# Four graph layers on one core: permuted graph in place, running sums on VectorE for slots and counts, un-permuting in three bfloat16 parts

## The chip, the core and the metric

The kernel runs on one core of one Trainium2 chip. The metric is the device time of one execution in microseconds (us), lower is better. The core has five engines that run side by side, each working through its own queue in order: TensorE (PE, matmuls into PSUM; its weight loads are listed as PEld), VectorE (DVE), ScalarE (ACT), GpSimd (POOL) and SyncE (SP, which here only starts DMAs). Before the change the median of three runs is 2626.49 us (2620.58 to 2630.43).

## What is computed

32 graphs of 512 nodes with 64 features (`x`, 32x512x64) and weighted, sparse adjacency matrices (`adj`, 32x512x512) go through four layers. Each adds its result to its input and normalizes over the 64 features:

```python
x = _layernorm(x + _L0_gnn_ref(x, adj))                    # mean over neighbours
x = _layernorm(x + _L1_gnn_ref(x, adj, weight, bias))      # Chebyshev terms of the Laplacian
x = _layernorm(x + _L2_gnn_ref(x, adj, att_W, att_b))      # hyperbolic attention of all pairs
x = _layernorm(x + _L3_gnn_ref(x, adj, nodemask, W1, b1, W2, b2))
```

The change touches layer 3. It first thins out the neighbour lists (`_dilate_adj`), then takes for every node and feature a weighted sum of three quantiles (0.25, 0.5, 0.75) over the values of the node's remaining neighbours, and last a small dense network:

```python
agg = _weighted_nanquantile_agg(x, adj_d > 0)
h = relu((x + agg) @ W1 + b1);  y = h @ W2 + b2
```

## The kernel before

The work of a graph is cut into lanes, and the lanes of many graphs are under way at a time. P is 128, N is 512 nodes, T = N/P = 4 blocks of rows, D is 64.

*front* (line 882) loads the adjacency, transposes it, and does layers 0 and 1. *pairs* and *tail* (lines 969 to 1145) do layer 2 on all pairs of nodes; the result is `x3`, split into three bfloat16 parts `x3h` (line 757). *graph* (lines 786 to 876) makes the thinned adjacency as a 0/1 matrix `V` in fp16 (lines 809 to 828), and then `order` ranks the nodes by their number of neighbours and permutes the columns of V into that ranking: `perm` is a one-hot matrix, and four groups of four matmuls (line 857) give VP, one block of 128 rows at a time, which ACT copies out of PSUM (line 858). Then come the *slots*: for each node its running number within each column, that is a sum over all rows above it. Block j takes j matmuls with a constant matrix (all 2) over the blocks above and one with a triangular matrix (lines 860 to 864), so 1 + 2 + 3 + 4 matmuls of 128x512. The *counts* (lines 865 to 867) are four more with a matrix of ones.

*gather* (line 1147) turns slots into one-hot matrices `oh` on DVE and multiplies them with `x3h` on PE, so that slot s of every node holds the features of its s-th neighbour; the values go to two long tiles, `SB` (BODY, the nodes with few neighbours) and `SH` (HEAD, 32 columns with many neighbours for a pair of graphs). *sort* and *head* (lines 1239 and 1270) run sorting networks over the slots, which are tensor_tensor instructions of min and max on DVE (line 448), multiply the sorted values with weights of the three quantiles and sum. The result, still in the ranking's order, is `ap` (fp32, two graphs in one tile, line 1267). *finish* (line 1315) undoes the ranking: one-hot matrices `PT` in fp32, made by two ACT instructions each (line 485), and four fp32 matmuls for a graph (line 1340), each of which appears as two instructions in the trace; `dense` (line 1346) does the small network. For the last two graphs `spots` (line 1296) makes the one-hots early, in tiles of the lane *pairs*.

What sets the order: no engine order is written by hand. A planner, the class `Order` (line 181), records every operation with an engine, a modelled duration and its dependences, and then simulates the five engines (`issue`, line 295). Whenever an engine is free it takes, of the operations whose inputs are there, the one with the earliest due time. Due times come from `STAGES` (line 1415): for each lane the first and last due time of its operations, in periods of 80 us after the graph's number times 80 us (line 1478). On PE an operation that needs another shape of the array than the one before (64 or 128 rows, 64 or 128 columns) is put back by `STAY` (line 188), 51.0 us of due time. Buffers are part of the plan: an operation that needs a tile waits until a buffer of its tag is free. The order found is then fixed for each engine. Where the plan has PE idle, padding matmuls of zeros (`stay_active`, line 1451) are put in.

The tiles concerned: in *graph* the tags `nbT` (then `perm`), `v` (then `VP`), `V` and `junk` have one buffer of 128x2048 or 128x512 fp16 each; `col` (line 707) gives small 128x4 columns with two buffers. `tt`, `ts` and `stt` (lines 447 to 455) are DVE instructions, `act` (line 477) ACT, `mm` (line 491) PE.

Of the kernel before, what the change touches and what calls it, by code (L numbers as in the profile page):

```python
# [20 lines left out]
P = 128  # L21
# [10 lines left out]
K = 24  # L32
# [148 lines left out]
class Order:  # L181
# [3 lines left out]

    ENGINES = ("PE", "DVE", "ACT", "POOL", "SP")
    HOP = 0.1
    STAY = 51.0

    def __init__(self, nc, tc):  # L190
        self.nc, self.tc = nc, tc
# [212 lines left out]
def tile_adj_resnorm(ctx: ExitStack, tc: tile.TileContext, x, adj, nodemask, w1k, b1k, att_w, att_b,  # L404
# [206 lines left out]
    onesb = const.tile([P, P], BF16, name="onesb")  # L611
    nc.vector.memset(onesb, 1.0)
    zero = const.tile([P, 2 * P], BF16, name="zero")
    nc.vector.memset(zero, 0.0)

    wk = const.tile([P, KO * D // P, D + 2], F32, name="wk")
# [88 lines left out]
        return a.unsqueeze(2).to_broadcast([P, T, n])  # L705

    def col(name):
        return seq.tile(pools["small"], [P, T], F32, name, 2)

    def wide(name, tag=None):  # L710
        return seq.tile(pools["small"], [P, T, D], F32, name, 1, tag)
# [118 lines left out]
    def order(b, res):  # L830

        gm = pools["gm"]
        V = res["V"]
        key = col("key")
        stt(key, M3[:, b, :], float(N), iotr, op0=OP.mult, op1=OP.add)
        pt = bank()
        for t in range(T):
            tr(pt[:, t * P:(t + 1) * P], key[:, t:t + 1].to_broadcast([P, P]), identf)
        keyh = col("keyh")
        ts(keyh, key, -0.5, None, op0=OP.add)  # L840
        sg = col("sg")
        for t in range(T):
            junk = seq.tile(gm, [P, N], F16, "junk", 1)
            act(junk, pt, AF.Sign, bias=keyh[:, t:t + 1], scale=-1.0, accum_out=sg[:, t:t + 1])
        rk = col("rk")
        ts(rk, sg, -0.5, 0.5 * N - 1.0, op0=OP.mult, op1=OP.add)

        rkh = seq.tile(pools["keep"], [P, T], F16, "rkh", 8)
        cp(rkh, rk)
        perm = seq.tile(gm, [P, T, N], F16, "perm", 1, "nbT")  # L850
        for t in range(T):
            ts(perm[:, t, :], iotap, rk[:, t:t + 1], None, op0=OP.is_equal)
        VP = seq.tile(gm, [P, T, N], F16, "VP", 1, "v")
        for j in range(T):
            pt = bank()
            for t in range(T):
                mm(pt, V[:, t, j * P:(j + 1) * P], perm[:, t, :], start=(t == 0), stop=(t == T - 1))
            act(VP[:, j, :], pt, AF.Copy)
        slot = seq.tile(pools["keep"], [P, T, N], F16, "slot", 2)
        for j in range(T):  # L860
            pt = bank()
            for k in range(j + 1):
                mm(pt, UC[:, :P] if k == j else UC[:, P:2 * P], VP[:, k, :], start=(k == 0), stop=(k == j))
            act(slot[:, j, :], pt, AF.Copy)
        pt = bank()
# [16 lines left out]
    def front(b, res):  # L882
# [69 lines left out]
        pt = bank()[:, :T * (D + 2)].rearrange("p (t n) -> p t n", n=D + 2)  # L952
        nu = KO * D // P
        for t in range(T):
            mm(pt[:, t, :], onesb, bias1, start=True, stop=False)
# [314 lines left out]
    def head(b, res):  # L1270
# [19 lines left out]
        for g in range(2):  # L1290
            mm(pt[P - CUT:, g * P:(g + 1) * P], PRS[:, g:g + n - 1:2], identf, start=True, stop=True)
        act(ap[P - CUT:, :, 1, :], pt[P - CUT:, :2 * P].rearrange("p (g c) -> p g c", g=2), AF.Copy)
        for g in range(2):
            finish(b - 1 + g, res["ends"][g], ap[:, g], res["spots"][g] if b == B - 1 else None)

    def spots(ends):

        mid = pools["mid"]
        seq.lane = "pairs"
        home = seq.tile(mid, [P, 4, N], F32, "ends", 1, "Q")  # L1300
        ones = [seq.tile(mid, [P, 4, N], F32, f"ones{g}", 1, tag) for g, tag in enumerate(("EX", "RW"))]
# [12 lines left out]

    def finish(b, end, ap, spot):
        rk, x3 = end
        if spot:
            ones, home = spot
            po = bank(home=home and "pairs")
            for u in range(2):  # L1320
                for h in range(2):
                    mm(po[h * D:(h + 1) * D, :], ap[:, u, h * D:(h + 1) * D], ones[:, 2 * h + u], start=(u == 0),
                       stop=(u == 1 and h == 1), pair=True)
# [9 lines left out]

        po = bank()
        for u in range(2):
            PT = seq.tile(pools["fin"], [P, 2, N], F32, "PT", 1)
            for h in range(2):
                onehot(PT[:, h, :], rr, nposc[:, 2 * h + u:2 * h + u + 1], pools["fin"])
            for h in range(2):
                mm(po[h * D:(h + 1) * D, :], ap[:, u, h * D:(h + 1) * D], PT[:, h, :], start=(u == 0),  # L1340
                   stop=(u == 1 and h == 1), pair=True)
# [4 lines left out]
    def dense(po, x3T, x3, dst, nm, home=None):  # L1346
# [12 lines left out]
        act(hT, ph[:HID, :], AF.Relu, bias=b1s)  # L1359
        py = bank(home=lane)[:, :T * D].rearrange("p (t n) -> p t n", n=D)  # L1360
        for t in range(T):
            mm(py[:, t, :], onesb, bias2, start=True, stop=False)
# [8 lines left out]
    limits = const.tile([B, 2, K + 1], F32, name="limits")  # L1371
# [12 lines left out]
    def within_bounds():  # L1384
# [17 lines left out]
        for i, op in enumerate((OP.is_gt, OP.is_lt)):  # L1402
# [300 lines left out]
```

## Time and profile before

| | |
|---|---|
| median of three runs (lowest, highest) | 2626.49 us (2620.58, 2630.43) |
| profiled execution: time, span | 2622.02 us, 2620.2 us |
| busy: PE, PEld | 2458.2 us (94%), 1635.4 us (62%) |
| busy: DVE, ACT, POOL | 2402.7 us (92%), 1879.2 us (72%), 815.8 us (31%) |
| granted PE clock, mean | 0.982 |
| padding matmuls of line 1453 | 973, 132.9 us |
| sorting network, SB and SH (line 448, DVE) | 565.8 us and 347.4 us |
| gather matmuls (PE) | 5376, 516.5 us |
| permuting, perm by V (PE) | 512, 141.0 us |
| slots, VP by UC, and counts, VP by onesP (PE) | 320, 91.2 us, and 128, 33.1 us |
| un-permuting, PT by ap (PE, fp32) | 240, 111.2 us |

How to read it: a group's line gives the source line (often that of a helper), the engine, the operation, the tiles written and read, their shapes, the count, the busy time in us and the mean length of one in ns, and then the idle time of the engine just before and what ended it. Busy times of groups that overlap can't be added. Tiles carry their lane's name in front: `graph_VP`, `head_PT`, `sort_ap`. The span is the time from the first to the last instruction of the profiled execution; 1.8 us lie around it.

### The profile page before, as it was taken

The page shows a single profiled execution, that of the slowest core. Times are in us where ns is not written, and L with a number is a line of the kernel's source. Part 1 is how long each engine was busy: PE and PEld are TensorE (multiplying, and loading weights), DVE is VectorE, ACT ScalarE, POOL GpSimd, SP SyncE. Part 2 cuts the span into 40 slices and gives each one's busy share as a digit, 9 for nine tenths or more (in the row PEclk, how much of TensorE's full clock was granted, in tenths as well). Part 3 has the DMA queues.
Part 4 walks back from the last instruction along what each step waited for, and adds up shares of the span by engine and source line. Part 5 has one row for each costly group of instructions (what it writes and reads, how often), then busy time and mean ns, then how long its engine had stood idle before and what let it go on. Part 6 is the DMA issues. An engine that isn't in the chain of part 4 may idle for free.

```text
span 2620.2 us, 55667 instructions
## 1 busy us (share of the span) xinstructions
PE 2458.2 (94%) x19641; PEld 1635.4 (62%) x19667; DVE 2402.7 (92%) x9002; ACT 1879.2 (72%) x4406; POOL 815.8 (31%) x1783
## 2 busy tenths in 40 slices
PE   7999999999999999999999999999999999999997
PEld 6666566666666666666656666566666666666655
DVE  3668998999999999999999999999999999998996
ACT  5666677767777777767777677777777778776761
POOL 1233332332343333322333233333323333332210
PEclk9999999999999999999999899999999999998999
DMA  1100000000000000000000000000000000000000
GB/s 38 33 23 21 17 14 15 25 22 23 18 11 22 20 25 21 24 17 13 20 21 25 19 19 13 20 23 22 26 19 13 18 19 26 19 11 3 5 7 8
DMA packets 119723, 49.96 MB, mean 19 GB/s; under 512 B 53740, under 2 KB 119436, under 8 KB 119436
## 3 DMA queue, kind: packets, MB, share of 16 engines
q1 hardware_dynamic: 118272, 46.15, 6.4%
q8 instruction: 156, 2.56, 0.4%
q14 instruction: 131, 1.07, 0.1%
q10 hardware_dynamic: 1164, 0.18, 0.0%
HBM read 37.93 MB, written 8.39 MB: 18 GB/s over the span
## 4 chain that ended last, share of the span: by engine, by line
DVE 72%; PE 18%; ACT 6%; issue 2%; POOL 2%; DMA 0%; ACTq 0%; DVEq 0%
DVE SB L448 17%; DVE SH L448 8%; DVE gather_oh L452 6%; PE front_bank L502 5%; DVE pairs_Q L448 4%; PE gather_bank L502 3%; PE graph_bank L502 3%; DVE pairs_RW L448 3%; PE pairs_bank L502 3%; DVE sort_prod L448 3%; DVE pairs_Wt L455 3%; DVE pairs_L L455 2%; DVE tail_v L448 2%; DVE pairs_EX L448 2%; DVE pairs_RW L455 2%
## 5 line engine op out<-in xcount | busy, mean ns | idle before, releaser
L448 DVE TENSOR_TENSOR SB<-SB 128x448 f32<-128x448 f32 (+11 forms) x1424 | 565.8, 424 | 12.2 <-ACT SB L483 0.7
L502 PE MATMUL gather_bank<-gather_oh,tail_x3h 128*64 128x448 f16 (+5 forms) x5376 | 516.5, 321 | 4.8 <-ACT SB L483 3.4
L502 PEld LDWEIGHTS <-tail_x3h 128*64 128x64 bf16 x5376 | 296.0, 111 | 214.3 <-issue 112.8
L448 DVE TENSOR_TENSOR SH<-SH 128x32 f32<-128x32 f32 (+11 forms) x1744 | 347.4, 246 | 8.1
L502 PE MATMUL pairs_bank<-pairs_FT 67*128 67x512 f32 (+7 forms) x768 | 316.9, 516 | 18.7 <-ACT pairs_EX L483 7.1
L452 DVE TENSOR_SCALAR gather_oh<-graph_slot 128x256 f16<-128x256 f16 (+9 forms) x864 | 252.3, 337 | 25.3 <-PE gather_bank L502 23.5
L502 PE MATMUL front_bank<-front_AT,front_y 128*64 128x512 f32 x768 | 189.5, 607 | 18.5 <-DVE front_y L448 17.0
L502 PEld LDWEIGHTS pairs_bank<-pairs_FT 67*128 67x128 f32 (+1 forms) x768 | 130.2, 194 | 83.2 <-issue 19.7
L502 PE MATMUL graph_bank<-graph_perm,graph_V 128*128 128x512 f16 x512 | 141.0, 382 | 16.1 <-DVE graph_perm L452 13.8
L502 PEld LDWEIGHTS <-graph_nbT 128*128 128x128 f16 x1536 | 113.1, 99 | 57.6 <-issue 17.3
L722 POOL TENSOR_TENSOR front_rs<-front_var,mhalf 128x4 f32<-128x4 f32 x64 | 83.4, 1303 | 201.8 <-DVE front_var L452 152.9
L502 PEld LDWEIGHTS front_bank<-XA,front_AT 128*128 128x128 f32 x1024 | 126.0, 194 | 13.6 <-issue 6.3
L1453 PE MATMUL PA<-zero 128*128 128x256 bf16 x973 | 132.9, 278 | 0.1
L502 PE MATMUL pairs_bank<-FLS,pairs_Wt 128*128 128x66 f32 x1024 | 124.7, 274 | 3.9 <-DVE pairs_Wt L455 3.8
L502 PEld LDWEIGHTS pairs_bank<-FLS,pairs_Wt 128*128 128x128 f32 x1024 | 120.6, 192 | 10.9 <-DVE pairs_Wt L455 7.8
L502 PE MATMUL front_bank<-XA,front_AT 128*128 128x65 f32 x1024 | 124.5, 274 | 0.0
L448 DVE TENSOR_TENSOR pairs_RW<-pairs_RW,pairs_EX 128x640 f32<-128x640 f32 x128 | 104.1, 815 | 18.7 <-ACT pairs_RW L483 18.4
L502 PEld LDWEIGHTS <-tabs 128*128 128x128 f16 x1296 | 78.3, 100 | 64.2 <-issue 54.9
L502 PEld LDWEIGHTS front_bank<-front_AT,front_y 128*64 128x64 f32 x768 | 54.5, 137 | 95.6 <-issue 63.0
L483 ACT ACTIVATE graph_VP<-graph_bank 128x512 f16<-128x512 f32 x128 | 75.5, 590 | 53.7 <-PE graph_bank L502 49.4
L483 ACT ACTIVATE SB<-gather_bank 128x448 f32<-128x448 f32 (+2 forms) x192 | 81.3, 438 | 43.4 <-PE gather_bank L502 43.0
L502 PE MATMUL head_bank<-head_PT,sort_ap 128*64 128x512 f32 x240 | 111.2, 608 | 0.1
(354 smaller groups left out, 6569.8 us busy)
## 6 DMA issues: line engine op xcount, KB each, us to landing
front_A<-in_adj_dram SPq DMA_DIRECT2D x128, 256.0 KB, 2.7
XA<-in_x_dram SPq DMA_DIRECT2D x32, 128.0 KB, 2.2
xs<-tail_x SPq DMA_DIRECT2D x32, 128.0 KB, 1.9
out_dram<-head_zo SPq DMA_DIRECT2D x31, 128.0 KB, 2.0
out_dram<-tail_ends SPq DMA_DIRECT2D x1, 128.0 KB, 2.1
wk<-in_L_gnn_weight_dram ACTq DMA_DIRECT2D x1, 64.0 KB, 3.0
w1s<-in_L_gnn_W_dram ACTq DMA_DIRECT2D x2, 32.0 KB, 2.0
attw<-in_L_gnn_att_W_dram ACTq DMA_DIRECT2D x2, 0.2 KB, 3.2
```

Source lines behind the costliest of these rows:

```text
L448: vec(lambda: nc.vector.tensor_tensor(out, a, b, op=op), out, [a, b])
L452: vec(lambda: nc.vector.tensor_scalar(out, a, s1, s2, op0=op0, **kw), out, [a], True, (s1, s2))
L455: vec(lambda: nc.vector.scalar_tensor_tensor(out, a, s, b, op0=op0, op1=op1), out, [a, b], False, (s,))
L483: 0.3, lambda: nc.scalar.activation(out, a, f, scale=scale, **kw), [out, accum_out], [a, after] + sc, table)
L502: return nc.tensor.matmul(out, w, a, start=start, stop=stop)
L722: seq.op("POOL", 0.8, 0.6, lambda: nc.gpsimd.tensor_tensor(y, v, mhalf, op=OP.pow), [y], [v])
L1453: return nc.tensor.matmul(PA[:, 2 * P:], zero[:, :P], zero, start=False, stop=False)
```

## The change

- **Permuted graph in place.** VP no longer has a tile: block j is written into the columns of V that the four matmuls of block j have just read. `perm` moves from nbT's buffer to v's.
- **Running sums.** The blocks above are summed on DVE in fp16 (into `junk`'s buffer, then into VP[0] and VP[1], which are no longer needed by then), so each slot block takes one matmul with the triangular matrix and at most one with the matrix of twos on the sum; the counts take one.
- **Un-permuting in three bfloat16 parts.** `ap` is split into three parts `aph` by three ACT copies and two DVE subtractions for a pair of graphs; PT and the early one-hots become fp16, and each fp32 matmul becomes three 16-bit ones. The operations no longer carry `pair=True`, which halved their modelled duration.
- **Room and small constants.** Twelve columns get one buffer in place of two; `onesb` gives way to `onesP`, `zero` is half as long and broadcast for padding; `limits` becomes fp16.
- **Planner.** `STAY` goes from 51.0 to 35.7, and all lanes get other due times.

```diff
-    STAY = 51.0
+    STAY = 35.7
...
-    zero = const.tile([P, 2 * P], BF16, name="zero")
+    zero = const.tile([P, P], BF16, name="zero")
...
     def col(name):
-        return seq.tile(pools["small"], [P, T], F32, name, 2)
+
+        once = name in ("two", "sq2", "al", "dn", "hx", "hx2", "rsn", "gam", "sn", "lp", "run", "uc")
+        return seq.tile(pools["small"], [P, T], F32, name, 1 if once else 2)
...
-        perm = seq.tile(gm, [P, T, N], F16, "perm", 1, "nbT")
+        perm = seq.tile(gm, [P, T, N], F16, "perm", 1, "v")
...
-        VP = seq.tile(gm, [P, T, N], F16, "VP", 1, "v")
+        def four(a):
+            return a.rearrange("p (t n) -> p t n", n=P)
+
+
+        VP = [V[:, :, j * P:(j + 1) * P] for j in range(T)]
...
-            act(VP[:, j, :], pt, AF.Copy)
+            act(VP[j], four(pt), AF.Copy)
...
+        sums = [None, VP[0], four(seq.tile(gm, [P, N], F16, "sums", 1, "junk")), VP[0], VP[1]]
         for j in range(T):
             pt = bank()
-            for k in range(j + 1):
-                mm(pt, UC[:, :P] if k == j else UC[:, P:2 * P], VP[:, k, :], start=(k == 0), stop=(k == j))
+            mm(four(pt), UC[:, :P], VP[j], start=True, stop=(j == 0))
+            if j:
+                mm(four(pt), UC[:, P:2 * P], sums[j], start=False, stop=True)
+                tt(sums[j + 1], sums[j], VP[j], op=OP.add)
             act(slot[:, j, :], pt, AF.Copy)
         pt = bank()
-        for k in range(T):
-            mm(pt, onesP, VP[:, k, :], start=(k == 0), stop=(k == T - 1))
+        mm(four(pt), onesP, sums[T], start=True, stop=True)
...
+        aph = seq.tile(pools["fin"], [P, 3, 2, 2, P], BF16, "aph", 1)
+        for q in range(3):
+            act(aph[:, q], ap, AF.Copy)
+            if q < 2:
+                tt(ap, ap, aph[:, q], op=OP.subtract)
         for g in range(2):
-            finish(b - 1 + g, res["ends"][g], ap[:, g], res["spots"][g] if b == B - 1 else None)
+            finish(b - 1 + g, res["ends"][g], aph[:, :, g], res["spots"][g] if b == B - 1 else None)
...
-            PT = seq.tile(pools["fin"], [P, 2, N], F32, "PT", 1)
+            PT = seq.tile(pools["fin"], [P, 2, N], F16, "PT", 1)
...
-            for h in range(2):
-                mm(po[h * D:(h + 1) * D, :], ap[:, u, h * D:(h + 1) * D], PT[:, h, :], start=(u == 0),
-                   stop=(u == 1 and h == 1), pair=True)
+            for q in range(3):
+                for h in range(2):
+                    mm(po[h * D:(h + 1) * D, :], ap[:, q, u, h * D:(h + 1) * D], PT[:, h, :], start=(u == 0 and q == 0),
+                       stop=(u == 1 and q == 2 and h == 1))
...
-    STAGES = {"front": (-0.6, -0.5), "pairs": (1.2, 1.3), "tail": (0.2, 1.5), "graph": (0.9, 1.0), "gather": (2.7, 2.9),
-              "sort": (4.5, 4.6), "head": (4.7, 5.6), "ends": (4.0, 4.5), "check": (3.4, 4.8)}
+    STAGES = {"front": (-0.7, -0.2), "pairs": (1.2, 1.4), "tail": (0.7, 1.2), "graph": (1.2, 1.5), "gather": (2.8, 3.3),
+              "sort": (4.8, 5.4), "head": (5.0, 6.0), "ends": (4.6, 4.8), "check": (2.6, 6.0)}
...
-                return nc.tensor.matmul(PA[:, 2 * P:], zero[:, :P], zero, start=False, stop=False)
+                return nc.tensor.matmul(PA[:, 2 * P:], zero, zero[:, 0:1].to_broadcast([P, 2 * P]), start=False, stop=False)
```

More of the change, by code (lines that the diff above doesn't have):

```diff
@@ L610, in tile_adj_resnorm @@
     nc.vector.memset(tiny, 1e-36)
-    onesb = const.tile([P, P], BF16, name="onesb")
-    nc.vector.memset(onesb, 1.0)
-    zero = const.tile([P, 2 * P], BF16, name="zero")
+    zero = const.tile([P, P], BF16, name="zero")
     nc.vector.memset(zero, 0.0)
@@ L954, in front @@
         for t in range(T):
-            mm(pt[:, t, :], onesb, bias1, start=True, stop=False)
+            mm(pt[:, t, :], onesP, bias1, start=True, stop=False)
             for u in range(nu):
@@ L1300, in spots @@
         home = seq.tile(mid, [P, 4, N], F32, "ends", 1, "Q")
-        ones = [seq.tile(mid, [P, 4, N], F32, f"ones{g}", 1, tag) for g, tag in enumerate(("EX", "RW"))]
+        ones = [seq.tile(mid, [P, 4, N], F16, f"ones{g}", 1, tag) for g, tag in enumerate(("EX", "RW"))]
         seq.lane = "tail"
@@ L1320, in finish @@
             for u in range(2):
-                for h in range(2):
-                    mm(po[h * D:(h + 1) * D, :], ap[:, u, h * D:(h + 1) * D], ones[:, 2 * h + u], start=(u == 0),
-                       stop=(u == 1 and h == 1), pair=True)
+                for q in range(3):
+                    for h in range(2):
+                        mm(po[h * D:(h + 1) * D, :], ap[:, q, u, h * D:(h + 1) * D], ones[:, 2 * h + u],
+                           start=(u == 0 and q == 0), stop=(u == 1 and q == 2 and h == 1))
             for t in range(T):
@@ L1335, in finish @@
         for u in range(2):
-            PT = seq.tile(pools["fin"], [P, 2, N], F32, "PT", 1)
+            PT = seq.tile(pools["fin"], [P, 2, N], F16, "PT", 1)
             for h in range(2):
                 onehot(PT[:, h, :], rr, nposc[:, 2 * h + u:2 * h + u + 1], pools["fin"])
-            for h in range(2):
-                mm(po[h * D:(h + 1) * D, :], ap[:, u, h * D:(h + 1) * D], PT[:, h, :], start=(u == 0),
-                   stop=(u == 1 and h == 1), pair=True)
+            for q in range(3):
+                for h in range(2):
+                    mm(po[h * D:(h + 1) * D, :], ap[:, q, u, h * D:(h + 1) * D], PT[:, h, :], start=(u == 0 and q == 0),
+                       stop=(u == 1 and q == 2 and h == 1))
         for t in range(T):
@@ L1361, in dense @@
         for t in range(T):
-            mm(py[:, t, :], onesb, bias2, start=True, stop=False)
+            mm(py[:, t, :], onesP, bias2, start=True, stop=False)
             mm(py[:, t, :], hT[:, t * P:(t + 1) * P], w2s, start=False, stop=True)
@@ L1370, in tile_adj_resnorm @@
     flag = const.tile([1, 1], I32, name="flag")
-    limits = const.tile([B, 2, K + 1], F32, name="limits")
+    limits = const.tile([B, 2, K + 1], F16, name="limits")
     for s in range(K + 1):
```

## The prediction

> **What bounds the kernel now.** I read the page's busy shares first, then the busy row of each engine, then the busy times in three stretches (filling of the pipeline, middle, end), then the waits inside the middle.
>
> ```profile
> PE 2458.2 (94%) x19641; PEld 1635.4 (62%) x19667; DVE 2402.7 (92%) x9002; ACT 1879.2 (72%) x4406; POOL 815.8 (31%) x1783
> ...
> PE   7999999999999999999999999999999999999997
> ...
> DVE  3668998999999999999999999999999999998996
> ```
>
> Two engines look full. PE's 94% holds something that isn't work: the matmuls of line 1453 are padding between the real ones. The answer by stretches, columns PE, PEld, DVE, ACT, POOL:
>
> ```profile
> 0.00:196.50 196.50, 177.22 (x1348) 130.00 (x1349) 106.43 (x394) 124.67 (x266) 46.47 (x182) 0.98 0.11 32
> 196.50:2489.00 2292.50, 2170.34 (x17328) 1431.76 (x17351) 2188.14 (x8130) 1700.69 (x4012) 754.03 (x1575) 0.98 0.07 19
> 2489.00:2620.20 131.20, 110.66 (x970) 73.66 (x970) 108.17 (x479) 53.85 (x128) 15.25 (x26) 0.95 0.03 8
> ```
>
> DVE idles 90.1 us while the pipeline fills, 104.4 in the middle (4.5%) and 23.0 at the end, 217.5 in all. In the middle PE idles 122.2 us, and the same stretches for line 1453 alone give 52.0 us of padding there (132.9 in the run): 174 us free (7.6%). So DVE is the tighter engine and PE a close second. Who waits for whom in the middle (us in total, times, longest):
>
> ```profile
> DVE gather_oh L452 <- PE gather_bank L502: 21.4, 16, 3.0
> DVE pairs_RW L448 <- ACT pairs_RW L483: 14.3, 13, 3.7
> DVE front_st L714 <- PE front_bank L502: 10.0, 24, 2.3
> DVE pairs_EX L455 <- PE pairs_bank L502: 6.7, 6, 3.2
> DVE pairs_L L455 <- PE pairs_bank L502: 6.3, 6, 1.8
> ```
>
> ```profile
> PE front_bank L502 <- DVE front_st L714: 20.7, 33, 1.9
> PE front_bank L502 <- DVE front_y L448: 15.2, 25, 1.9
> PE graph_bank L502 <- DVE graph_perm L452: 13.4, 20, 1.3
> ```
>
> Each waits for the other, in many short waits. All lines of the first list that name PE add up to 51 us, those that name ACT or POOL to 30; the rest of the 104 is gaps too small to be listed. The chain that ended last says the same:
>
> ```profile
> DVE 72%; PE 18%; ACT 6%; issue 2%; POOL 2%; DMA 0%; ACTq 0%; DVEq 0%
> ```
>
> [...] 24 gather matmuls of 448 columns at 64 output rows take 2.46 us near the end, 0.10 each[...]
>
> **The change, part by part.** Prices, by shape (busy, mean ns):
>
> ```profile
> L502 PE MATMUL graph_bank<-graph_VP,UC 128*128 128x512 f16 x320 | 91.2, 383 | 2.6 <-ACT graph_VP L483 1.9 <-ACT graph_slot L483 0.5
> L502 PE MATMUL head_bank<-head_PT,sort_ap 128*64 128x512 f32 x240 | 111.2, 608 | 0.1
> L448 DVE TENSOR_TENSOR pairs_Q<-pairs_RW 128x512 f32<-128x512 f32 x32 | 21.8, 680 | 0.1
> L448 DVE TENSOR_TENSOR gather_oh<-graph_slot,last 128x512 f16<-128x512 f16 x32 | 13.3, 414 | 0.0
> ```
>
> Instructions overlap, so a duration isn't what one takes from its engine. The timeline of DVE shows by how much (start, length):
>
> ```profile
> 1277.32 0.41 DVE L448 TENSOR_TENSOR graph_nbT<-graph_nbT,identb 128x512 f16<-128x512 f16 x1
> 1277.66 0.64 DVE L448 TENSOR_TENSOR SH<-SH 128x14 f32<-128x14 f32 x4
> ```
>
> The next starts 0.34 us after an fp16 sum of 0.41 us; after the fp32 one of the pairs stage at 1304.82 it starts 0.58 us later. On PE four 128x512 fp16 matmuls in a row (the counts, at 331.66) take 1.03 us where one takes 0.38, so 0.22 us each.
>
> *Running sums on DVE (added).* Three fp16 sums of 512 elements for each of 32 graphs, 96 x 0.34 = 32.6 us. *Splitting ap into three parts (added).* Two fp32 subtractions of 512 elements for each of 16 pairs of graphs, 32 x 0.60 = 19.2 us (0.60: between 0.58 and the 0.68 of the row). DVE gets 51.8 us more, to 2454. Nothing is taken off DVE. Bounds: 45 if subtractions hide better, 62 with whole durations.
>
> *Slots and counts (removed from PE).* Matmuls per graph go from 1+2+3+4 plus 4 to 1+2+2+2 plus 1, 14 to 8: 6 x 0.22 x 32 = 42 us. *Un-permuting (changed on PE).* The fp32 row is 240 instructions in 111 us for 30 graphs, 3.7 us of busy time each, some of it overlap of ends. Twelve 16-bit matmuls of 512 columns take its place: 1.4 us if the halves run side by side (12 x 0.10 x 512/448), 2.6 if not (12 x 0.22). Saved: 1.1 to 2.3 us a graph; I take 1.1, since the two halves become ready apart, so 33 us. PE loses 75 us together (60 to 110).
>
> *ACT (added).* Three copies of 512 elements for each pair; the nearest row, head_PT's write from SBUF, is 628 ns: 48 x 0.63 = 30 us, on an engine that is busy 72%. Covered: free time of 592 us in the middle; without that cover 30 us. The one-hots in fp16 keep their 512 elements, so nothing there.
>
> *New waits.* The matmuls of slots 1 to 3 and of the counts now wait for ACT's copy and a DVE sum; behind them on PE lies whatever the planner put there. Each sum waits for ACT's copy of a block with the rest of DVE's queue behind it; so does each subtraction. That is 5 places a graph where DVE can stall; the listed waits of the middle are now 91, with 81 us. Bounds: 0 (planned where inputs are long there) to 13 us (96 sums and 32 subtractions x 0.1); I take 5.
>
> *End.* For the last two graphs nothing hides the splitting: three copies and two subtractions in a chain, 3 x 0.63 + 2 x 0.68 + about 0.8 for four hand-overs = 4 us, less 0.5 us of cheaper matmuls: +3.5 us, inside the stretch that now idles 23.
>
> *Buffers, STAY and STAGES.* perm moves into v's buffer and VP into V's, so nbT is free a step earlier and V later; the graph stage is rarely waited for by DVE (graph_v 1.4, graph_key 0.8, graph_mi 0.8, graph_nbT 0.4 us in the middle), so at most 3 us gained; I take none. Twelve small columns lose their second buffer: 0 to 10 us, I take none. The planner's numbers change the whole order: a lower STAY means more changes of tile shape on PE, other due times move waits about. No row shows it; bounds are minus 30 us (a third of the middle's idle time) and plus 30; I take 0. The filling of the pipeline hangs on the first graph's latency (gather starts at 183 us on PE), which no part shortens: 90 us of idle time stay. The smaller constants (onesP, zero, limits) cost nothing: the same instruction counts.
>
> *What comes back.* A lighter PE answers earlier. PE loses 75 of some 2325 us of real work, and DVE waits for PE 51 us in the middle; as DVE always has more queued work than before, I take back half of these waits and a little: 30 us.
>
> Sum: 2622.0 (the profiled execution: span 2620.2 and 1.8 around it) + 51.8 + 5 + 3.5 - 30 = 2652; the chain of waits gives a second reading: 51.8 x 72/92 = 40 added along DVE's part, 75 x 18/94 = 14 taken from PE's, 30 x 6/72 = 2 for ACT, so +28 and 2650 with 2622. The profiled execution lies inside the runs (2620.6 to 2630.4), 4.5 us below the median of 2626.5. I forecast **2650 us**, 0.9% slower than the median.
>
> **Rivals.** *PE paces, and DVE's idle time collapses (faster).* DVE would have 2454 us of work plus 90 + 23 + 4 at the ends. With 30 us of idle time in the middle the time is 2454 + 117 + 30 + 2 = 2603. It decides from 40 us down (2613): more than six tenths of the middle's idle time must go. For it: 51 us of it are waits for PE, and stretches with little idle time exist. Against it: PE waits for DVE longer than DVE for PE, and the 30 us for ACT and POOL and the small gaps stay. *Exactly as much comes back as is added (no change):* idle time of 40 to 65 us in the middle, about 2625. *The new order scatters the waits:* the middle's idle time grows to 130 us: 2454 + 117 + 130 + 2 = 2703; for it speak the single buffers, the new waits, and that a plan made on modelled durations is fragile when one engine is nearly full. *The sums don't do what they should:* if the block views keep fp16 at single rate, each costs 0.60 like fp32, 96 x 0.26 = 25 us more: 2675.
>
> **How the numbers follow.** Forecast (2640 to 2665) 0.36; PE paces 0.28; no change 0.22; scattered 0.09; single rate 0.05. This measurement can tell about 0.5% from no change, that is 2613 to 2640. Faster 0.28, same 0.22, slower 0.36 + 0.09 + 0.05 = 0.50. The range of 2592 to 2690 leaves out a tenth below (an order that is also better) and a tenth above. The slower cases alone span 2640 to 2703.
>
> **What would show it.** In the profile after: DVE busy near 2454 and x9130; three fp16 sums a graph at about 414 ns and subtractions near 680; 96 matmuls less in the slots (x224) and 96 less in the counts (x32); no fp32 rows with ap; DVE's share in the middle at 96% or more. If the waits on gather_bank, front_bank and pairs_bank nearly vanish and DVE reaches 98%, the first rival holds. If DVE's busy time is right but its share falls, the order did it. A DVE busy time that does not grow by 45 to 62 us would break the first step.

## The result, and the profile after

The median after the change is 2600.78 us over four runs (2598.72 to 2604.69), against 2626.39 us over four runs of the kernel before (2620.58 to 2630.43). The ratio is 0.9906, 95% interval 0.9884 to 0.9928: faster by about 0.9%. The forecast was 2650 us, slower by 0.9%; the time lies inside the range of 2592 to 2690 and close to the first rival's 2603.

The profiled execution took 2600.4 us, its span is 2598.0 us, 22.2 less than before. The busy shares of the page after, and DVE's busy row:

```profile
PE 2431.4 (94%) x19596; PEld 1606.4 (62%) x19626; DVE 2438.0 (94%) x9129; ACT 1915.9 (74%) x4464; POOL 825.5 (32%) x1783
...
DVE  3669999999999999999999999999999999999996
```

DVE has 127 instructions and 35.3 us more, and its row has lost the 8s in the middle. The stretches (columns: length, then PE, PEld, DVE, ACT, POOL with their counts, then the granted PE clock, DMA share, GB/s):

```profile
0.00:196.50 196.50, 179.32 (x1371) 131.21 (x1373) 108.04 (x411) 124.64 (x268) 49.29 (x185) 1.00 0.12 32
196.50:2469.00 2272.50, 2147.90 (x17287) 1400.24 (x17310) 2224.42 (x8261) 1741.39 (x4087) 759.92 (x1576) 0.99 0.07 19
2469.00:2598.00 129.00, 104.16 (x942) 74.93 (x943) 105.50 (x459) 49.84 (x113) 16.25 (x24) 0.93 0.03 8
```

Length minus busy time gives DVE's idle time: 88.5, 48.1 and 23.5 us, where it was 90.1, 104.4 and 23.0. So the span's 22.2 us are 35.3 more of work and 57.4 less of idle time, and 56.3 of those are in the middle, where DVE is now busy 97.9%. Who DVE waits for in the middle, the three longest:

```profile
DVE front_st L714 <- PE front_bank L502: 8.1, 20, 0.6
DVE gather_oh L452 <- PE gather_bank L502: 6.1, 5, 2.2
DVE pairs_L L455 <- PE pairs_bank L502: 5.3, 4, 2.3
```

These three were 10.0, 21.4 and 6.3 us, and the waits for ACT in `pairs_RW` (14.3) and for `pairs_EX` (6.7) have gone from the head of the list. Of PE's waits for DVE these two have become longer (they were 15.2 and 13.4):

```profile
PE front_bank L502 <- DVE front_y L448: 22.8, 42, 1.5
PE graph_bank L502 <- DVE graph_perm L452: 20.5, 27, 1.5
```

The chain of work that ended last has moved to DVE as well (it was 72% DVE, 18% PE):

```profile
DVE 83%; PE 10%; ACT 2%; issue 2%; POOL 2%; DMA 0%; ACTq 0%; DVEq 0%
```

The groups of the new work, by shape:

```profile
L502 PE MATMUL head_bank<-head_PT,head_aph 128*64 128x512 f16 x360 | 87.0, 393 | 1.9 <-ACT head_PT L483 1.6
...
L502 PE MATMUL graph_bank<-graph_V,UC 128*128 128x512 f16 x192 | 63.3, 383 | 0.5 <-ACT graph_V L483 0.4
...
L502 PE MATMUL graph_bank<-graph_V,onesP 128*128 128x512 f16 x32 | 12.3, 384 | 0.0
...
L502 PE MATMUL graph_bank<-graph_sums,UC 128*128 128x512 f16 x32 | 12.1, 379 | 0.0
```

```profile
L483 ACT ACTIVATE head_aph<-sort_ap 128x512 bf16<-128x512 f32 x48 | 30.1, 627 | 7.9 <-DVE sort_ap L448 7.7
...
L448 DVE TENSOR_TENSOR sort_ap<-sort_ap,head_aph 128x512 f32<-128x512 f32 x32 | 21.8, 680 | 2.6 <-ACT head_aph L483 2.6
...
L448 DVE TENSOR_TENSOR graph_V<-graph_V 128x512 f16<-128x512 f16 x32 | 13.3, 415 | 0.0
L448 DVE TENSOR_TENSOR graph_V<-graph_sums,graph_V 128x512 f16<-128x512 f16 x32 | 13.2, 413 | 0.0
L448 DVE TENSOR_TENSOR graph_sums<-graph_V 128x512 f16<-128x512 f16 x32 | 13.2, 412 | 4.4 <-ACT graph_V L483 4.4
```

The work is there as announced, at the announced durations. What doesn't fit the forecast is the 56 us of idle time that went.

**A quantity the prediction left out: the granted clock.** The two traces record PE's clock at half speed in 14 stretches of 3.4 to 17.1 us before and in 11 of 3.4 to 13.7 us after, and at full speed for the rest. From the mean clocks, 0.9819 and 0.9882, they sum up to 2 x 0.0181 x 2620 = 95 us before and 61 us after. It matters here: in three series of 24 to 27 runs of the kernel before, its time falls by 18.7, 17.0 and 18.1 us for each 0.01 of mean clock (correlation -0.97 to -0.98). I use 18 us per 0.01 below to set runs beside each other "at equal clock". That is an estimate from a correlation, good to a few us. For the two profiled executions it says: of 21.6 us, 0.006 of clock go with 10.8, and 11 remain. Why the clock was higher in the kernel after is not shown by any run.

### The profile page after: what moved, and what is told of

It is laid out like the page before. It is cut to its first block, busy times and chain, and to the rows that moved or that the text cites. A ratio compares the mean times of both kernels' runs of the same rounds, so it can differ in the third digit from the quotient of the medians.

```text
span 2598.0 us, 55822 instructions
## 1 busy us (share of the span) xinstructions
PE 2431.4 (94%) x19596; PEld 1606.4 (62%) x19626; DVE 2438.0 (94%) x9129; ACT 1915.9 (74%) x4464; POOL 825.5 (32%) x1783
## 4 chain that ended last, share of the span: by engine, by line
DVE 83%; PE 10%; ACT 2%; issue 2%; POOL 2%; DMA 0%; ACTq 0%; DVEq 0%
DVE SB L448 19%; DVE SH L448 11%; DVE gather_oh L452 7%; DVE pairs_Q L448 4%; DVE sort_prod L448 3%; DVE pairs_RW L448 3%; DVE pairs_Wt L455 3%; PE front_bank L502 3%; DVE pairs_L L455 2%; DVE tail_v L448 2%; PE pairs_bank L502 2%; DVE pairs_EX L455 2%; DVE pairs_RW L455 2%; DVE pairs_EX L448 2%; PE gather_bank L502 1%
## 5 line engine op out<-in xcount | busy, mean ns | idle before, releaser
L502 PE MATMUL gather_bank<-gather_oh,tail_x3h 128*64 128x448 f16 (+5 forms) x5376 | 548.6, 321 | 4.9 <-ACT SB L483 2.3
L448 DVE TENSOR_TENSOR SH<-SH 128x32 f32<-128x32 f32 (+10 forms) x1744 | 347.7, 246 | 6.1
L502 PE MATMUL pairs_bank<-pairs_FT 67*128 67x512 f32 (+7 forms) x768 | 310.0, 510 | 16.8 <-DVE pairs_L L455 10.0
L483 ACT ACTIVATE graph_V<-graph_bank 128x512 f16<-128x512 f32 x256 | 151.1, 590 | 72.9 <-PE graph_bank L502 71.0
L502 PEld LDWEIGHTS <-graph_nbT 128*128 128x128 f16 x1536 | 115.6, 99 | 58.2 <-issue 18.8
L722 POOL TENSOR_TENSOR front_rs<-front_var,mhalf 128x4 f32<-128x4 f32 x64 | 89.1, 1393 | 163.4 <-DVE front_var L452 130.0
L502 PE MATMUL pairs_bank<-FLS,pairs_Wt 128*128 128x66 f32 x1024 | 137.0, 274 | 0.7 <-DVE pairs_Wt L455 0.5
L483 ACT ACTIVATE graph_v<-graph_bank,graph_c 128x512 f16<-128x512 f32 x128 | 87.8, 686 | 62.1 <-PE graph_bank L502 46.5
L502 PE MATMUL front_bank<-XA,front_AT 128*128 128x65 f32 x1024 | 132.9, 273 | 0.1
L483 ACT ACTIVATE graph_junk<-graph_bank,graph_keyh 128x512 f16<-128x512 f32 x128 | 87.5, 683 | 32.9 <-PE graph_bank L507 25.6
L502 PEld LDWEIGHTS front_bank<-fold,front_sums 128*128 128x128 f32 x768 | 98.3, 192 | 21.2 <-issue 5.4
```

The costliest lines, as they stand in the source:

```text
L448: vec(lambda: nc.vector.tensor_tensor(out, a, b, op=op), out, [a, b])
L483: 0.3, lambda: nc.scalar.activation(out, a, f, scale=scale, **kw), [out, accum_out], [a, after] + sc, table)
L502: return nc.tensor.matmul(out, w, a, start=start, stop=stop)
L722: seq.op("POOL", 0.8, 0.6, lambda: nc.gpsimd.tensor_tensor(y, v, mhalf, op=OP.pow), [y], [v])
```

## The experiments

Two theories stood against each other. *Load*: the work moved off PE made PE answer earlier, and DVE's waits closed (the first rival). *Order*: the lighter PE brings nothing, DVE pays in full for its new work, and the gain is the planner's new numbers, `STAY` and `STAGES`. In all tables the ratio is to the kernel before on the same chip, with its 95% interval; "at equal clock" is the difference of mean times to before, corrected as above; "idle" is DVE's idle time in the middle (from 196.5 us to 130 us ahead of the span's end), which was 104.4 before and 48.1 after.

### Numbers and work, crossed

*old_work_new_numbers* is the kernel before with the change's numbers; the other three are the changed kernel with old numbers put back, both or one of the two.

*old_work_new_numbers*, on the kernel before:

```diff
-    STAY = 51.0
+    STAY = 35.7
-    STAGES = {"front": (-0.6, -0.5), "pairs": (1.2, 1.3), ...
+    STAGES = {"front": (-0.7, -0.2), "pairs": (1.2, 1.4), ...
```

On the changed kernel, the same lines the other way round: both in *new_work_old_numbers*, `STAY` alone in *new_work_old_stay*, `STAGES` alone in *new_work_old_stages*.

> The kernel before with STAY and STAGES of the kernel after, its work unchanged. If the planner's numbers took the idle time out of DVE (order theory), DVE keeps 2403 us of work, idles some 50 us in the middle and 113 at the two ends: about 2568 us. If the lighter PE did it (load theory), PE is as full as before and the time stays at 2615 to 2640 us.

> The kernel after with STAY and STAGES of the kernel before. Order theory: DVE has 2438 us of work and idles 104 us in the middle as before: about 2655 us. Load theory: the time stays near that of the change, 2595 to 2610 us.

> The kernel after with STAY at 51.0 again and nothing else. If STAY is the part of the order that counts: 2630 us or more, and some 400 changes of tile shape less on PE in the middle. If the due times are that part, or if it is the load: 2595 to 2610 us.

> The kernel after with the STAGES of before and nothing else. If the due times are the part of the order that counts: 2630 us or more. If STAY is that part, or if it is the load: 2595 to 2610 us.

| | median us | ratio (95%) | clock | at equal clock | DVE busy | idle |
|---|---|---|---|---|---|---|
| before, same chip | 2617.26 | 1 | 0.985 | 0 | | |
| old_work_new_numbers | 2610.55 | 0.9970 (0.9956 to 0.9985) | 0.986 | -5 us | 2408.5 | 87.2 |
| new_work_old_numbers | 2680.16 | 1.0223 (1.0188 to 1.0257) | 0.980 | +53 us | 2455.9 | 105.9 |
| new_work_old_stay | 2623.71 | 1.0023 (0.9999 to 1.0047) | 0.981 | -1 us | 2445.2 | 73.5 |
| new_work_old_stages | 2733.87 | 1.0423 (1.0388 to 1.0458) | 0.986 | +116 us | 2465.4 | 151.8 |

The moved work, with the old numbers, costs 63 us by the medians and 58 by the ratio. (It comes with the smaller buffers and the permuted graph in place, and with a plan of its own; no run takes the buffers back alone.) DVE's busy time grows by 53.2 and its idle time in the middle stays (105.9 for 104.4): a PE with less real work has not shortened it. The trace of *new_work_old_numbers*, middle stretch, then its longest wait, then the two lines of padding of the whole run:

```profile
196.50:2547.80 2351.30, 2193.71 (x18036) 1487.21 (x18050) 2245.40 (x8301) 1746.19 (x4080) 765.00 (x1577) 0.98 0.07 18
```

```profile
DVE gather_oh L452 <- PE gather_bank L502: 38.6, 26, 3.4
```

```profile
L1468 PE MATMUL PA<-zero 128*128 128x256 bf16 x1521 | 210.1, 281 | 0.1
...
L1469 PE MATMUL PA<-UC,identb 128*128 128x256 f16 x392 | 50.8, 273 | 1.5 <-ACT sort_ap L483 1.4
```

The wait for `gather_bank` is longer than before (21.4), and all waits of DVE for PE in the middle add up to 52 us, as before (54). The padding has gone from 132.9 to 210.1 us in the first line and from 14.1 to 50.8 in the second, which the prediction had left out: more than was taken from PE has come back as padding, which fits a DVE that, with more to do, keeps PE waiting. So *load* falls. But *order* doesn't stand in its simple form either. By the ratios the same numbers are worth 83 us (64 at equal clock) on the new work and 8 (5) on the old, where I had expected a large gain. And `STAY` and `STAGES` can't be priced apart: with the new `STAGES` the new `STAY` gains, with the old ones it makes the slowest kernel of all, whose longest wait is again this one (from 196.5 to 2450 us):

```profile
DVE gather_oh L452 <- PE gather_bank L502: 63.2, 36, 3.4
```

What is left is that the numbers are *fitted* to the work they were found with. The next runs test that.

### Numbers fitted to each work, and the two parts one at a time

For *old_work_fitted_numbers* I searched the numbers with the planner itself, for the old work; for *new_work_fitted_numbers* in the same way for the new. *new_numbers_sums_on_pe* and *new_numbers_fp32_unpermute* take one part back out of the change and leave its numbers.

*old_work_fitted_numbers*, on the kernel before:

```diff
+    STAY = 52.1
+    STAGES = {"front": (-0.8, 0.42), "pairs": (1.2, 1.4), "tail": (0.96, 1.04), "graph": (1.2, 1.5), "gather": (3.1, 3.13),
+              "sort": (4.73, 5.45), "head": (5.14, 6.15), "ends": (4.6, 4.8), "check": (2.63, 6.6)}
```

*new_work_fitted_numbers*, on the changed kernel:

```diff
+    STAY = 40.8
+    STAGES = {"front": (-0.7, -0.12), "pairs": (1.2, 1.4), "tail": (0.68, 1.55), "graph": (1.2, 1.5), "gather": (2.8, 3.3),
+              "sort": (4.84, 5.31), "head": (5.36, 6.93), "ends": (4.6, 4.8), "check": (2.25, 6.02)}
```

*new_numbers_sums_on_pe*, on the changed kernel:

```diff
-            mm(four(pt), UC[:, :P], VP[j], start=True, stop=(j == 0))
-            if j:
-                mm(four(pt), UC[:, P:2 * P], sums[j], start=False, stop=True)
-                tt(sums[j + 1], sums[j], VP[j], op=OP.add)
+            for k in range(j + 1):
+                mm(four(pt), UC[:, :P] if k == j else UC[:, P:2 * P], VP[k], start=(k == 0), stop=(k == j))
...
-        mm(four(pt), onesP, sums[T], start=True, stop=True)
+        for k in range(T):
+            mm(four(pt), onesP, VP[k], start=(k == 0), stop=(k == T - 1))
```

*new_numbers_fp32_unpermute*, on the changed kernel:

```diff
-        aph = seq.tile(pools["fin"], [P, 3, 2, 2, P], BF16, "aph", 1)
-        for q in range(3):
-            act(aph[:, q], ap, AF.Copy)
-            if q < 2:
-                tt(ap, ap, aph[:, q], op=OP.subtract)
...
+            PT = seq.tile(pools["fin"], [P, 2, N], F32, "PT", 1)
...
+                mm(po[h * D:(h + 1) * D, :], ap[:, u, h * D:(h + 1) * D], PT[:, h, :], start=(u == 0),
+                   stop=(u == 1 and h == 1), pair=True)
...
```

> The work of the kernel before, unchanged, with STAY and due times searched for it with the planner itself. Fit theory (the gain of the change comes from numbers that fit its work; the moved work costs time): DVE keeps about 2405 us and idles 50 to 70 us in the middle, 2575 to 2590 us, faster than the change. Room theory (only with work taken off PE can DVE be kept fed): not under 2605 us however the numbers are chosen.

> The kernel after with STAY and due times searched further in the same manner. Fit theory: a little faster than the change, about 2585 us, since less idle time is left in DVE; not faster than the old work with its own numbers by more than the 35 us of DVE work that the change adds would let it. Room theory: 2585 us too, and clearly faster than the old work with fitted numbers.

> The kernel after with slots and counts as 14 matmuls on PE again, the rest as after. DVE loses 33 us of work, PE gets 42. Room theory: DVE waits for PE again, 2625 us or more. Fit theory: the due times fit this work as little as any other, so somewhere from 2590 to 2650; DVE's busy time falls to about 2405 us.

> The kernel after with ap and the one-hots in fp32 again and two fp32 matmul pairs with the halved modelled duration, the rest as after. DVE loses 19 us, ACT 30, PE gets about 25. Room theory: 2615 us or more. Fit theory: 2580 to 2600 us, DVE's busy time about 2419.

| | median us | ratio (95%) | clock | at equal clock | DVE busy | idle |
|---|---|---|---|---|---|---|
| before, same chip | 2615.99 | 1 | 0.986 | 0 | | |
| old_work_fitted_numbers | 2575.29 | 0.9839 (0.9797 to 0.9880) | 0.981 | -49 us | 2389.5 | 72.7 |
| new_work_fitted_numbers | 2604.31 | 0.9954 (0.9939 to 0.9968) | 0.982 | -18 us | 2436.2 | 54.2 |
| new_numbers_sums_on_pe | 2633.82 | 1.0063 (1.0045 to 1.0082) | 0.984 | +14 us | 2423.3 | 96.6 |
| new_numbers_fp32_unpermute | 2594.82 | 0.9917 (0.9891 to 0.9944) | 0.987 | -20 us | 2425.4 | 55.9 |

The old work with numbers of its own is faster than the changed kernel (0.9839 against 0.9906, intervals just apart; -49 against -11 us at equal clock), with nothing moved between engines. Its middle:

```profile
196.50:2447.70 2251.20, 2151.40 (x17220) 1415.43 (x17220) 2178.46 (x8135) 1690.93 (x4020) 761.63 (x1579) 0.98 0.07 19
```

72.7 us idle instead of 104.4, with the 9002 instructions of before. *new_work_fitted_numbers* is a miss: it was to beat the change and is slower, though at a lower clock (0.982 for 0.988); at equal clock it is 7 us ahead, which is about what the estimate can resolve. Here the planner, which works on modelled durations, found numbers that took 1.6% off the old work, but did not rank two kernels half a per cent apart. The two single parts are read with care, since taking a part out re-plans everything: without the running sums the change's numbers lose 1.6%, though 96 instructions of DVE and 14.7 us of its busy time are gone; without the three parts they lose nothing (0.9917 against 0.9906). The first can be read as the same misfit as above, and then says nothing on the worth of the sums; the second shows that the numbers don't misfit every other work. For a price, the order has to be held.

### The order held, one cost changed

In three of the next four kernels the planner doesn't know of the edit, so that every queue keeps its order. *sums_twice_same_order* issues each running sum twice; *counts_seven_times_same_order* issues the counts' matmul seven times (192 more, 192 x 0.22 = 42 us of PE); *old_order_fewer_matmuls* leaves out, in the kernel before, six of the 14 slot and count matmuls of each graph, as many as the change saves, and with them the sums over the blocks further up. *graph_due_earlier* does the reverse: the changed work untouched, one due time of nine moved by 0.1 period (8 us).

*sums_twice_same_order*, on the changed kernel:

```diff
+    def tt2(out, a, b, op):
+        def go():
+            nc.vector.tensor_tensor(out, a, b, op=op)
+            return nc.vector.tensor_tensor(out, a, b, op=op)
+        vec(go, out, [a, b])
...
-                tt(sums[j + 1], sums[j], VP[j], op=OP.add)
+                tt2(sums[j + 1], sums[j], VP[j], op=OP.add)
```

*counts_seven_times_same_order*, on the changed kernel:

```diff
+            for _ in range(times - 1):
+                nc.tensor.matmul(out, w, a, start=start, stop=stop)
             return nc.tensor.matmul(out, w, a, start=start, stop=stop)
...
-        mm(four(pt), onesP, sums[T], start=True, stop=True)
+        mm(four(pt), onesP, sums[T], start=True, stop=True, times=7)
```

*old_order_fewer_matmuls*, on the kernel before:

```diff
+            if skip:
+                return None
             return nc.tensor.matmul(out, w, a, start=start, stop=stop)
...
+                mm(..., start=(k == max(j - 1, 0)), stop=(k == j), skip=(k < j - 1))
...
+            mm(..., start=(k == T - 1), stop=(k == T - 1), skip=(k < T - 1))
```

*graph_due_earlier*, on the changed kernel:

```diff
-    STAGES = {..., "graph": (1.2, 1.5), ...
+    STAGES = {..., "graph": (1.1, 1.5), ...
```

> The kernel after, its order kept, with each of the 96 running sums on DVE issued twice (the second, unplanned, writes the same values): 33 us more work on DVE and nothing else. If DVE paces at this order: 25 to 33 us longer than the change, about 2630. If its 48 us of idle time in the middle take work up: 2600 to 2610 us.

> The kernel after, its order kept, with the one matmul of the counts issued seven times for each graph, unplanned: 192 x 0.22 = 42 us more on PE, as much as the running sums took off it. Room theory: PE's relief is what the change lives on, so 20 us or more are lost. Fit theory: DVE paces and PE has 176 us of padding and idle time in the middle, so 10 us or less.

> The kernel before, its order kept, with 6 of the 14 matmuls of slots and counts of each graph not issued (the sums over the blocks further up are left out): 42 us less on PE, nothing more on DVE. Room theory: DVE's waits for PE shrink, 20 us or more gained. Fit theory: some 10 us gained, since DVE waits for a place in the order and not for PE's total.

> The kernel after with the first due time of the graph lane at 1.1 instead of 1.2 periods (8 us), nothing else. Fit theory: the order is fragile, so one small number can cost as much as the whole change moves: 2640 us or more, with DVE's idle time in the middle up and its work as it was. Room theory: DVE has slack for such a shift, 2590 to 2610 us.

| | median us | ratio (95%) | clock | at equal clock | DVE busy | idle |
|---|---|---|---|---|---|---|
| before, same chip | 2619.44 | 1 | 0.983 | 0 | | |
| sums_twice_same_order | 2633.85 | 1.0056 (1.0032 to 1.0079) | 0.988 | +23 us | 2475.4 | 45.8 |
| counts_seven_times_same_order | 2604.19 | 0.9946 (0.9928 to 0.9963) | 0.992 | +1 us | 2440.0 | 50.5 |
| old_order_fewer_matmuls | 2620.53 | 1.0004 (0.9991 to 1.0018) | 0.975 | -15 us | 2403.5 | 105.0 |
| graph_due_earlier | 2663.84 | 1.0174 (1.0138 to 1.0209) | 0.989 | +55 us | 2452.4 | 101.3 |

The middle stretches of the four, in the order of the table:

```profile
196.50:2499.90 2303.40, 2149.78 (x17310) 1398.49 (x17307) 2257.64 (x8347) 1742.40 (x4085) 754.99 (x1576) 0.99 0.07 19
```

```profile
196.50:2472.50 2276.00, 2171.84 (x17493) 1409.10 (x17491) 2225.46 (x8259) 1742.46 (x4085) 755.04 (x1576) 1.00 0.07 19
```

```profile
196.50:2489.50 2293.00, 2152.72 (x17166) 1425.82 (x17163) 2188.04 (x8118) 1698.98 (x4010) 748.90 (x1572) 0.97 0.07 19
```

```profile
196.50:2534.90 2338.40, 2200.70 (x17817) 1456.31 (x17816) 2237.07 (x8253) 1735.82 (x4071) 739.60 (x1568) 0.99 0.07 18
```

*DVE paces one to one*, in the order of the changed kernel. 37.4 us more of DVE busy time (2475.4 less 2438.0) cost 1.5% against the change's own ratio, 39 us (34 at equal clock), and the idle time stays where it was.

*PE's load hardly matters.* Added up by their starts in the traces, the matmuls of the graph lane take 39 us more of PE and 41 us less, near the 42 planned. 42 us more on PE cost 0.40% (10 us), 12 at equal clock; PE had about 170 us free in the middle there (124.6 idle, 45.8 of padding; I had written 176). 42 us less on PE, in the order of before, bring nothing at all (1.0004): DVE's idle time is 105.0 for 104.4, and its longest wait is unchanged:

```profile
DVE gather_oh L454 <- PE gather_bank L506: 21.8, 19, 3.1
```

I had expected some 10 us here. The clock column shows where they may have gone: over 20 runs the mean clock is 0.975 where before has 0.983, which by the slope is worth 15 us. So by this estimate 42 us of PE are worth 12 us (added, in the new order) to 15 us (removed, in the old one), about a third. In both held orders the clock followed the number of matmuls: fewer went with 0.975 for 0.983, more with 0.992 for 0.988, which gives part of the effect back. That the number of matmuls sets the clock would fit both runs, but is not shown: no run holds the matmuls and changes the clock alone. It isn't PE's idle time in sum that decides: in *sums_twice_same_order* PE idles 153.6 us of the middle, 29 more than in the changed kernel, at the same clock.

*One due time is worth 2.7%.* The same work as the change, with 8 us of due time moved in one lane, is at 1.0174 instead of 0.9906, and slower than before: DVE's idle time in the middle is 101.3 us for 48.1. Neither part of the change reaches that in any comparison here at fitted numbers or in a held order: the order outweighs the work.

### Each part with numbers of its own

What stayed open was whether either part is worth something once the numbers suit it. Both kernels were given numbers searched for them.

*sums_fp32_fitted_numbers*, the changed kernel with fp32 un-permuting, running sums kept:

```diff
+    STAY = 55.2
+    STAGES = {"front": (-0.89, 0.44), "pairs": (1.2, 1.4), "tail": (0.62, 1.38), "graph": (1.2, 1.5), "gather": (3.13, 3.25),
+              "sort": (4.37, 5.66), "head": (5.17, 6.11), "ends": (4.7, 4.73), "check": (3.27, 6.79)}
```

*parts_fitted_numbers*, the changed kernel with slots and counts on PE, three parts kept:

```diff
+    STAY = 32.2
+    STAGES = {"front": (-0.98, 0.53), "pairs": (1.2, 1.4), "tail": (0.55, 0.65), "graph": (1.2, 1.5), "gather": (3.13, 3.15),
+              "sort": (4.37, 5.49), "head": (5.43, 6.61), "ends": (4.77, 4.79), "check": (2.68, 6.95)}
```

> Running sums and V in place, but ap and one-hots in fp32 as before, with numbers searched for this work. If the running sums are worth something once the numbers fit: below 2570 us, that is below the old work with fitted numbers (0.984 of before). If they are worth nothing or cost: 2575 to 2600 us.

> Un-permuting in three parts and V in place, but slots and counts on PE as before, with numbers searched for this work (0.992 of before was the fp32 un-permuting with the change's numbers, 1.006 this work with them). If fit is what counts, this misfit of 2634 us goes down to 2575 to 2600 us with its work unchanged. If PE's load counts, it stays above 2610.

| | median us | ratio (95%) | clock | at equal clock | DVE busy | idle |
|---|---|---|---|---|---|---|
| before, same chip | 2623.51 | 1 | 0.983 | 0 | | |
| sums_fp32_fitted_numbers | 2583.02 | 0.9846 (0.9822 to 0.9870) | 0.982 | -43 us | 2415.1 | 60.3 |
| parts_fitted_numbers | 2568.28 | 0.9805 (0.9779 to 0.9832) | 0.989 | -42 us | 2410.9 | 41.7 |

*parts_fitted_numbers* is the fastest kernel of the study, 1.95% under before and about 1% under the change. Its middle:

```profile
196.50:2434.40 2237.90, 2118.71 (x17279) 1404.08 (x17290) 2196.21 (x8151) 1711.20 (x4059) 723.38 (x1570) 0.99 0.07 19
```

Set beside the old work with fitted numbers (0.9839), the running sums show no gain (0.9846), and the three parts at most a little: 0.9805 and 0.9839 have overlapping intervals, and at equal clock the difference is gone (-42 and -49). Both kernels also carry the permuted graph in place and the smaller buffers, whose worth no run takes apart, and nothing shows that the three searches went equally deep; so what a part is worth at its best numbers stays open within about half a per cent.

## Why the prediction was wrong, step by step

The direction was wrong: 0.9% faster, not slower. Two terms of the sum failed; the others held, with the remarks below.

- **"The planner's numbers change the whole order ... I take 0", bounds minus 30 to plus 30.** This is the term that turned the sign. Measured on the new work it is -83 us (-64 at equal clock), far outside its bounds. In the two traces, of 79.8 us of span 57.8 are DVE's idle time in the middle and 17.9 its busy time for the same 9129 instructions. I had bounded it by a third of the middle's idle time; the change took away 56 us of it against before, and 58 against its own work with the old numbers. I also gave each edit its own term, though the numbers have no size of their own: 8 us on the old work, 83 on the new.
- **"What comes back ... 30 us".** Wrong too, with the opposite sign of error: with the old numbers nothing came back (idle 105.9 for 104.4). Without this term the sum for the moved work is 51.8 + 5 + 3.5 = 60.3 us; *new_work_old_numbers* measured 58 to 63. So for the work alone the sum was right, and the return that I took off was not there. That it came out within a few us is in part luck: this kernel too has a plan of its own, and plans differ by far more here.
- **The clock** was in no term. After minus before, 0.006 of it go with 10.8 us. Where these 0.006 come from stays open. It isn't simply fewer gaps on PE: *old_work_fitted_numbers* has the fewest in the middle (99.8 us idle) and a mean clock of 0.981.
- **DVE +51.8 us.** The rows are as priced: 680 ns for the fp32 subtractions and 412 to 415 ns for the fp16 sums, in the block views as well (so no "single rate", an fp16 sum that takes as long as an fp32 one), and taking overlaps off by the trace's starts the sums occupy 32.5 us and the subtractions 19.4, together 51.9. The page's total grew only by 35.3, and by the test I had named (45 to 62) the step would have failed. The rest lies in the other 9002 instructions, about 16 us less. Their total depends on the order: the kernel before and three others with the same 9002 lie between 2389.5 and 2408.5, and the change's 9129 between 2436.2 and 2465.4. By the trace about half of the 16 is more overlap of neighbours (8.8 us) and half shorter single instructions (8.0); why these are shorter is not shown.
- **PE minus 75 us.** Counts came out (x192 plus x32, and x32), and slots and counts save 37 us of busy time for 42. The un-permuting saves 24, not 33. But PE's total fell only by 26.8, since others grew: the gather matmuls of 256 and 196 columns by 18.8 and 11.5 us (their rows follow). The lower `STAY` allows more changes of tile shape: by the shapes of the recorded matmuls there are 1258 in the middle for 880 (1039 with the old `STAY` and all else as after), and a matmul behind one starts about 95 ns later, set against the end of the one before it, than others do. Over the 16 kernels traced here, the busy time of all gather matmuls rises with these changes, from 500.4 us at 800 to 549.4 at 1259 (correlation 0.95, 84 ns for each). So this is probably what a change of tile shape costs PE, for which the prediction had no row; that is an estimate from the 95 ns and the 84 ns, and no run varies the number of changes alone.
- **New waits +5.** DVE waits 4.4 us ahead of the running sums, once and in the filling, and 2.6 ahead of the subtractions at the end; neither has a wait in the middle, where I had put them.
- **ACT +30, end +3.5.** ACT grew by 36.7, covered as said: DVE's waits for ACT in the middle fell from 22.9 us to 0.6. The end's idle time went from 23.0 to 23.5. The splitting of the last pair took 3.4 us for 4 (2573.39 to 2576.79 in the trace): its four hand-overs between ACT and DVE cost 0.03 to 0.04 us each, and the 0.8 for all four was an estimate that no row had shown.

The gather rows of the kernel after, by shape (busy us, mean ns of one):

```profile
L502 PE MATMUL gather_bank<-gather_oh,tail_x3h 128*64 128x256 f16 x768 | 87.2, 284 | 1.7 <-ACT tail_x3h L483 1.1 <-ACT SH L483 0.5
...
L502 PE MATMUL gather_bank<-gather_oh,tail_x3h 128*64 128x196 f16 x768 | 57.7, 254 | 0.0
```

The same rows before:

```profile
L502 PE MATMUL gather_bank<-gather_oh,tail_x3h 128*64 128x256 f16 x768 | 68.4, 288 | 1.2 <-ACT tail_x3h L483 1.2
...
L502 PE MATMUL gather_bank<-gather_oh,tail_x3h 128*64 128x196 f16 x768 | 46.2, 251 | 0.0
```

Matmuls of about the same length (284 ns for 288, 254 for 251) take more of PE's time together (87.2 us for 68.4, 57.7 for 46.2), so they overlap less.

**The rival that hit the time did so by luck.** "PE paces, and DVE's idle time collapses" gave 2603, and both its signs came: DVE at 97.9% of the middle, the three waits for PE at 19.5 us in place of 37.7. Yet *old_order_fewer_matmuls* takes the 42 us off PE and nothing collapses, and *new_work_old_numbers* takes all of it off and the waits for PE stay at 52 us, the longest growing to 38.6. The signs I had named could not tell an engine that answers earlier from an order that asks later. The rival "scattered" (2703) was closer in kind: its mechanism, order, with a reach of some 100 us, decided the result, though with the other sign.

## What to carry to other kernels

When a change moves work and also retunes the numbers that order it, price the two apart, and give the order the widest bounds: here 8 us in one due time moved the kernel by 2.7%, and tuned numbers kept 8 of their 83 us on the old work. To learn what an engine's time is worth, hold the order and double one operation behind the planner's back; a comparison in which everything is re-planned measures the fit of the numbers. And before moving work to another engine to relieve a busy one, compare two prices taken in that way: here a microsecond on DVE cost one, and a microsecond off PE brought nothing as measured and about a third at equal clock.

## What was not expected of the hardware

- Time at half clock goes with nearly all of the scatter between runs of the kernel before (correlation -0.97 to -0.98): 18 us per 0.01 of mean clock, though PE is busy 94% with padding in its gaps.
- Removing 192 matmuls (42 us) from a fixed order went with a mean clock of 0.975 for 0.983, and adding 192 with 0.992 where the changed kernel has 0.988; in the first case no gain was left, and by the slope above the clock accounts for all of it.
- DVE's busy time for the same instructions varied by up to 29 us from order to order (2436.2 to 2465.4), so a difference of two page totals is not the cost of an added group.
